# Four graph-attention layers in float32: the tokens of most steps transposed by VectorE in 32x32 blocks after a move across partitions by DMA

## The chip, the core and the metric

The kernel runs on one core of one Trainium2 chip. Five engines work from their own queues, in order: TensorE (PE in the profile; its weight loads are PEld), VectorE (DVE), ScalarE (ACT), GpSimd (POOL) and SyncE (SP), which here only issues DMAs. The metric is the device time of one execution in microseconds; lower is better.

## The reference

There are 8192 tokens of 512 features: 128 graphs of 64 nodes, each graph with its own 64x64 adjacency. Four layers follow each other, each of this form:

```python
h = jnp.maximum(_layernorm(x, axis=-1), 0.0)
x = x + gnn_layer(h, adj, ...)
```

Layers 0 and 2 are attention with 4 heads of 64 (`q = h @ Wq`, `k = h @ Wk`, `v = h @ Wv`, a masked softmax over the 64 nodes of a graph, `out @ Wo + bo`). Layer 1 first normalizes `h` once more with `gamma` and `beta`, and has 8 heads of 64. Layer 3 maps `h` by `map_w`, takes queries and keys from the result, masks the softmax by the cosine similarity of the mapped tokens, and applies it to tokens mapped by another matrix. All of it is float32.

## The kernel before

Work goes in steps of 512 tokens (TB = 4 blocks of 128), 16 steps to a layer, 64 in all; a step is named (l, s). The matrix products want the tokens with features on partitions and tokens along the free axis. A step passes through these stages:

- `loads` (L470): two DMAs of 256 tokens each bring x from DRAM into a tile xin [128 tokens, 2 blocks, 512]; xin has four such tiles (L248). A load of layer l waits for the store of layer l-1 at the same step. SP issues it at L484.
- `layernorms` (L494), one stream for each half: statistics on VectorE (L443, L445), a power on GpSimd (L450), the normalization with ReLU on ScalarE (L459), in place. Layer 1 does this twice.
- `transposes` (L525): TensorE turns 128x128 pieces into PSUM (tile ptr, L539; L516 in layer 1), four pieces to a bank, and ScalarE copies the bank into hT [128 features, 4 chunks, 512 tokens] (L544; in layer 1 L521, which also applies gamma and beta). The xin tile is free when its last transpose is done. There are two hT tiles. Then `has_h` (L557) takes one of the three tiles t [128, 4, 2, 256] for sums of quarters of hT, which GpSimd makes (`sums_of_b`, L356, instruction L366).
- `projections` (L701): each product of a step with a weight matrix is a `winograd` (L633): seven products of quarters in place of eight, on PE at L585, into the PSUM tiles mA, mB, mC. ScalarE evicts (L602, L606, L622), VectorE adds (L615, L626). hT and t are free when all projections that use them are done.
- `scores`, `softmax`, `transposed` (L890 to L953): PE at L902, then VectorE, ScalarE and GpSimd; the probabilities are turned by ScalarE copies of 32-row pieces (L946) and one VectorE transpose in 32x32 blocks (L951).
- `attention` (L1047): PE at L1069, an eviction into a tile of the bank m (L1078), quarter sums by VectorE in another tile of t (L363, called oT_T in the code), and the output product, whose parts are added to the residual. That is read again from DRAM into xres (L992), gets the bias on GpSimd (L996) and the product by L1012 with L1017 or by L615, and is stored at L1037.
- Layer 3 has its own end: `norms` (L828) sends the squared lengths through DRAM and back by small DMAs (L853, L860, L867, L877), and `last` (L1195) multiplies at L1214, adds at L1121 and stores at L1126; its residuals come in at L1107.

All stages are Python generators. A list scheduler (class `Order`, L93) runs them while the program is built: each `yield` names an engine, a duration and a latency, for instance `pe(0.115)` for a transpose or `("sp", 0.6, 3.9)` for a load. It always takes the operation that can start first, and at equal times the stream with the lower priority number (stores 0, attention and residuals 2, transposes 3, loads and layernorms 4, projections 5); it lets urgent streams pass on ACT and DVE. Events hold a stream until something is done, `Ring` hands out tiles in turn, `Bank` gives any free tile to the first who asks. The order of instructions on each engine is fixed by this plan; on the chip an instruction waits for its inputs, and everything behind it on its engine waits too.

The lines that the change touches are mainly these:

```python
pt, pe_ = yield from r_tr.new("ptr")
for c in range(NC):
    yield pe(0.115)
    nc.tensor.transpose(pt[:, c, :], x[:, t, c * P:(c + 1) * P], ident)
```

Of the kernel before, what the change touches and what calls it, by code (L numbers as in the profile page):

```python
# [14 lines left out]
P = 128  # L15
D = 512
N = 64
TB = 4
# [210 lines left out]
def gnn_stack(ctx: ExitStack, tc: tile.TileContext, a: dict, out: bass.AP):  # L229
# [15 lines left out]
    soft = ctx.enter_context(tc.tile_pool(name="soft", bufs=3))  # L245
    dram = ctx.enter_context(tc.tile_pool(name="dram", bufs=1, space=bass.MemoryType.DRAM))
    r_w = ring("w", 4, [P, 7, 2, H])
    r_xin = ring("xin", 4, [P, 2, D])  # L248
    r_xres = ring("xres", 2, [P, 2, D])
    r_u = bank("u", 4, [P, D])  # L250
    r_h = ring("h", 2, [P, NC, TB * P])
# [213 lines left out]

        return lambda j, k: v[:, 2 * j:2 * j + 2, k * H:(k + 1) * H]

    loaded, l_ready = {}, {}

    def loads(steps):  # L470
        for l, s in steps:
            if l > 0:
                yield x_done[l - 1, s]
            for half in range(2):
                v, e = yield from r_xin.new()
                loaded[l, s, half] = v, e

                if (l, s) == (0, 1):
                    if half == 0:
                        yield begun_w  # L480
                    yield ("actq", 0.5, 0.0)
                else:
                    yield load(3.9)
                (nc.scalar if (l, s) == (0, 1) else nc.sync).dma_start(  # L484
                    v, x_of(l, s)[half * H:(half + 1) * H, :].rearrange("(t p) d -> p t d", p=P))
                if (l, s) == (0, 1):
                    if half == 1:
                        loads_begun.set()
                    yield ("actq", 0.0, 8.0)
                l_ready[l, s, half].set()  # L490
# [3 lines left out]
    def layernorms(steps, half):  # L494

        for l, s in steps:
            yield l_ready[l, s, half]
            x, xe = loaded.pop((l, s, half))
            rs = yield from scales(x)
            yield from normalize(x, rs, AF.Relu)  # L500
            if l == 1:
                rs = yield from scales(x)
                yield from normalize(x, rs, AF.Identity)
            normed[l, s, half] = x, xe
            n_ready[l, s, half].set()

    def scaled_chunks(s, h):

        for half in range(2):
            yield n_ready[1, s, half]  # L510
        x = [normed.pop((1, s, half)) for half in range(2)]
        for c in range(NC):
            pt, pe_ = yield from r_tr.new("ptr")
            for b in range(TB):
                yield pe(0.115)
                nc.tensor.transpose(pt[:, b, :], x[b // 2][0][:, b % 2, c * P:(c + 1) * P], ident)  # L516
            if c == NC - 1:
                for _, xe in x:
                    xe.set()
            yield act(0.6)  # L520
            nc.scalar.activation(h[:, c, :], pt.rearrange("p b k -> p (b k)"), AF.Identity,  # L521
                                 bias=beta[:, c:c + 1], scale=gamma[:, c:c + 1])
            pe_.set()

    def transposes(steps):  # L525

        for l, s in steps:
            h, h_done[l, s] = yield from r_h.new("hT")
            hT[l, s] = h
            if l == 1:  # L530
                yield from scaled_chunks(s, h)
            for half in range(2 if l != 1 else 0):
                yield n_ready[l, s, half]
                x, xe = normed.pop((l, s, half))
                for t in range(2):
                    pt, pe_ = yield from r_tr.new("ptr")
                    for c in range(NC):
                        yield pe(0.115)
                        nc.tensor.transpose(pt[:, c, :], x[:, t, c * P:(c + 1) * P], ident)  # L539
                    if t == 1:  # L540
                        xe.set()
                    yield act(0.6)
                    b = 2 * half + t
                    nc.scalar.copy(h[:, :, b * P:(b + 1) * P], pt)  # L544
                    pe_.set()
                if (l, s, half) == (0, 0, 0):
                    yield from has_h(l, s, h)
            if (l, s) == (3, 1):
                yield o_taken
            if (l, s) != (0, 0):  # L550
                yield from has_h(l, s, h)
            yield from sums_of_b(quarters(h), hB[l, s][1], (l, s) == (0, 0))
            hB[l, s][2].set()
            if (l, s) == (0, 0):
                first_t.set()
# [688 lines left out]

    steps = [(l, s) for l in range(4) for s in range(NG)]
    for k in steps:
        for e in (p_ready, s_ready, p_used, h_ready, x_done):
            e[k] = od.event()
        for half in range(2):
            l_ready[(*k, half)], n_ready[(*k, half)] = od.event(), od.event()  # L1250
    with tc.manual_schedule():
        od.spawn(weights(), 4)
        od.spawn(loads(steps), 4)
        for half in range(2):
            od.spawn(layernorms(steps, half), 4)
        od.spawn(transposes(steps), 3)
        od.spawn(projections([k for k in steps if k[0] < 3]), 5)
        od.spawn(fronts(steps), 1)
        od.spawn(turns(steps), 1)
        od.spawn(attentions(steps), 2)  # L1260
        od.run()
# [45 lines left out]
```

## Time and profile before

| | |
|---|---|
| median of 3 runs | 2819.91 us (2817.82 to 2821.3) |
| profiled execution | 2823.6 us, span 2821.8 us |
| PE busy | 2766.3 us (98%), 27176 matmuls |
| DVE busy | 1822.2 us (65%) |
| ACT busy | 1679.4 us (60%) |
| POOL busy | 1539.3 us (55%) |
| DMA | 238.56 MB in 160433 packets, 85 GB/s on average |
| transposes of tokens on PE | L539 x768, L516 x256 |
| granted TensorE clock | 0.995 of full speed |

Busy time is the time in which an engine has an instruction under way; matmuls are pipelined, so a busy PE is not a PE at its peak. The span is that of the profiled execution, from its first instruction to its last. DMA packets are single contiguous pieces; a share of 1 in a window would be all 16 DMA engines busy throughout it. Layer 0 lies at about 0 to 466 us of the span, layer 1 from there to 1400, layer 2 to 1850 and layer 3 to the end; neighbouring layers overlap a little.

### The profile page before, as it was taken

What the parts mean: (1) busy time and instruction counts of PE and PEld (TensorE: products, weight loads), DVE (VectorE), ACT (ScalarE), POOL (GpSimd) and SP (SyncE); (2) the same over time, 40 slices, a digit from 0 to 9 for tenths busy, and PEclk for the clock granted to TensorE, in tenths of its full rate; (3) what the DMA queues carried; (4) which work ended last, traced back from release to release, by engine and by line L of the source; (5) the groups of instructions that cost most, each with busy time, mean ns of one, the idle gap of its engine ahead of it and who ended that gap; (6) DMA issues with size and microseconds to landing.
All of it is one profiled execution on the core that took longest, in us unless ns stands there. A gap on an engine that the chain in (4) does not pass through costs nothing.

```text
span 2821.8 us, 64271 instructions
## 1 busy us (share of the span) xinstructions
PE 2766.3 (98%) x27176; PEld 2398.8 (85%) x27176; DVE 1822.2 (65%) x2724; ACT 1679.4 (60%) x2841; POOL 1539.3 (55%) x1158
## 2 busy tenths in 40 slices
PE   8999999999999999999999999999999999999997
PEld 7888888888888888888889888888888888888876
DVE  6776676776665666655756667646666666665557
ACT  5666666667555755755656657655555555555444
POOL 5676667553444443335565576686545545455443
PEclk9999999999999999999999999999999999999998
DMA  4243233220211111212242233333222322222221
GB/s 156 92 136 100 98 114 129 80 91 29 80 46 69 54 61 47 76 61 77 79 136 99 99 122 107 107 121 85 70 63 82 88 77 62 63 78 75 65 63 46
DMA packets 160433, 238.56 MB, mean 85 GB/s; under 512 B 23953, under 2 KB 69009, under 8 KB 160145
## 3 DMA queue, kind: packets, MB, share of 16 engines
q1 hardware_dynamic: 145632, 219.98, 24.5%
q10 hardware_dynamic: 14512, 14.47, 1.6%
q8 instruction: 214, 3.51, 0.5%
q14 instruction: 75, 0.61, 0.1%
HBM read 166.77 MB, written 67.63 MB: 83 GB/s over the span
## 4 chain that ended last, share of the span: by engine, by line
PE 90%; DVE 4%; POOL 3%; ACT 1%; issue 1%; DMA 1%; POOLq 0%; ACTq 0%; SPq 0%; DVEq 0%
PE mA L585 44%; PE mC L585 22%; PE mB L585 11%; PE sc L902 5%; PE ptr L539 3%; PE po L1069 2%; PE po L1214 1%; PE ptr L516 1%; ACT F L946 1%; POOL t L366 1%; POOL xres L996 1%; PE mmn L844 1%; DVE t L363 1%; POOL E L937 1%; POOL xres L1017 1%
## 5 line engine op out<-in xcount | busy, mean ns | idle before, releaser
L946 ACT COPY F<-E 32x512 f32<-32x512 f32 x768 | 472.5, 615 | 53.7 <-POOL E L937 43.0
L1017 POOL TENSOR_TENSOR xres<-xres,u 128x512 f32<-128x512 f32 x192 | 249.3, 1305 | 207.1 <-ACT u L1012 162.5
L996 POOL TENSOR_TENSOR xres<-xres,u 128x512 f32<-128x512 f32 x192 | 257.0, 1360 | 88.3 <-DMA xres<-x 41.1
L459 ACT ACTIVATE xin<-xin,rs 128x512 f32<-128x512 f32 x320 | 248.6, 811 | 16.7 <-DVE rs L452 15.0
L366 POOL TENSOR_TENSOR t<-hT 128x512 f32<-128x512 f32 x126 | 170.6, 1354 | 144.0 <-ACT hT L544 82.8
L937 POOL TENSOR_TENSOR E<-E,sm 128x1024 f32<-128x1024 f32 x64 | 128.4, 2006 | 201.3 <-DVE sm L935 156.2
L443 DVE BATCH_NORM_STATS2 st<-xin 128x6 f32<-128x512 f32 x320 | 215.2, 672 | 30.1 <-DMA xin<-x 14.3
L602 ACT COPY v<-mA 128x256 f32<-128x256 f32 (+1 forms) x192 | 92.1, 480 | 215.6 <-PE mA L585 201.5
L450 POOL TENSOR_TENSOR rs<-rs,mhalf 128x2 f32<-128x2 f32 x160 | 122.9, 770 | 170.4 <-DVE rs L448 128.8
L585 PE MATMUL mA<-w_vo,t 128*128 128x128 f32 (+1 forms) x1152 | 204.6, 311 | 0.8 <-ACT v L602 0.6
L366 POOL TENSOR_TENSOR t<-hT,t 128x512 f32<-128x512 f32 x126 | 169.7, 1347 | 35.4 <-ACT hT L521 32.2
L585 PE MATMUL mA<-t,w_qk 128*128 128x256 f32 x768 | 185.2, 380 | 2.4 <-DVE t L363 1.4
L931 DVE TENSOR_REDUCE sm<-E 128x16 f32<-128x1024 f32 x128 | 155.2, 1212 | 42.3 <-ACT E L924 41.7
L585 PE MATMUL mA<-t,w_q 128*128 128x256 f32 x744 | 181.2, 380 | 0.9 <-ACT qT L602 0.9
L585 PEld LDWEIGHTS mA<-w_vo,t 128*128 128x128 f32 x1152 | 166.5, 191 | 13.0 <-ACT u L1012 1.8
L585 PE MATMUL mA<-t,w_k 128*128 128x256 f32 x744 | 177.4, 381 | 0.0
L585 PEld LDWEIGHTS mA<-t,w_qk 128*128 128x128 f32 x768 | 142.9, 190 | 21.2 <-issue 1.7
L585 PEld LDWEIGHTS mA<-t,w_k 128*128 128x128 f32 x744 | 140.3, 190 | 19.3
L585 PEld LDWEIGHTS mA<-t,w_q 128*128 128x128 f32 x744 | 137.7, 190 | 20.2 <-issue 2.5
L951 DVE STREAM_TRANSPOSE pt<-F 128x1024 f32<-128x1024 f32 x96 | 118.6, 1235 | 50.5 <-ACT F L946 50.4
L1012 ACT COPY u<-mA 128x512 f32<-128x512 f32 x144 | 84.4, 586 | 107.9 <-PE mA L585 102.2
L937 POOL TENSOR_TENSOR E<-E,f 128x1024 f32<-128x1024 f32 x32 | 63.8, 1994 | 129.9 <-DVE nz L965 65.0
(216 smaller groups left out, 6863.7 us busy)
## 6 DMA issues: line engine op xcount, KB each, us to landing
x<-xres SPq DMA_DIRECT2D x96, 512.0 KB
xin<-x SPq DMA_DIRECT2D x96, 512.0 KB
xres<-x SPq DMA_DIRECT2D x64, 512.0 KB
xres<-in_x SPq DMA_DIRECT2D x32, 512.0 KB
u<-rs SPq DMA_DIRECT2D x128, 128.0 KB
xres<-x SPq DMA_DIRECT2D x64, 256.0 KB
out<-xres SPq DMA_DIRECT2D x64, 256.0 KB
xin<-in_x SPq DMA_DIRECT2D x30, 512.0 KB
```

Source lines behind the costliest of these rows:

```text
L366: nc.gpsimd.tensor_tensor(o, i0, i1, ALU.subtract)
L443: nc.vector.bn_stats(st, v[:, t, :])
L450: nc.gpsimd.tensor_tensor(rs[:, 0, :], rs[:, 1, :], mhalf[:, :2], ALU.pow)
L459: nc.scalar.activation(v[:, t, :], v[:, t, :], func, bias=rs[:, 2, t:t + 1], scale=rs[:, 0, t:t + 1])
L585: nc.tensor.matmul(o, l, r, start=(first and m == 0 and k == 0), stop=(k == KC - 1), skip_group_check=True)
L902: nc.tensor.matmul(S[g * N:(g + 1) * N, par, col], lT[r, c, k], rT[r, c, k], start=True, stop=True)
L931: nc.vector.tensor_reduce(o, E, AX.X, ALU.add)
L937: nc.gpsimd.tensor_mul(E, E, sm[:, :, None].to_broadcast([P, 16, N]))
L946: nc.scalar.copy(F[g * N + 32 * k:g * N + 32 * (k + 1), :, 32 * i:32 * (i + 1)], E[g * N + 32 * i:g * N + 32 * (i + 1), :, 32 * k:32 * (k ...
L951: nc.vector.transpose(o, F)
L996: nc.gpsimd.tensor_add(xr[:, t, :], xr[:, t, :], bo[l])
L1017: nc.gpsimd.tensor_add(v, v, both(u))
```

## The change

In steps 2 to 15 of layers 1, 2 and 3 (42 of the 64 steps) the tokens are no longer transposed by TensorE. Instead:

- A new stream `moves` (priority 3) waits until both halves of a step are normalized, takes a tile t, and issues 16 DMAs on SP from xin into that tile (called F in this role). Each takes 32 partitions and, of each of the 16 pairs of token block and feature chunk, 32 contiguous floats, 128 bytes; it changes the place of a 32x32 block among partitions and columns. The plan counts 0.45 us of SP for each, and 8 us from the issue of the last until it has landed. xin is free after them. In layer 3 an hT tile is taken ahead of the moves; in layers 1 and 2 only when the step is turned.
- `turned_tokens`, called from the stream `transposes`, waits for the moves and turns F into hT with two VectorE transposes in 32x32 blocks, of two token blocks (1024 columns) each.
- In layer 1 ScalarE then applies gamma and beta in place in hT (`scaled`), four instructions of 512 columns.
- The quarter sums of hT are then written into the same tile t over F, by GpSimd as before.
- xin becomes two tiles of four blocks instead of four of two, the same memory; both halves of a step share one.

Steps 0 and 1 of each layer, and all of layer 0, keep the transposes on TensorE.

```diff
-    r_xin = ring("xin", 4, [P, 2, D])
+    r_xin = ring("xin", 2, [P, TB, D])
...
+    by_blocks = [(1, 2), (1, 3), ... (3, 14), (3, 15)]
...
-                v, e = yield from r_xin.new()
-                loaded[l, s, half] = v, e
+                if half == 0:
+                    x, e = yield from r_xin.new()
+                v = x[:, 2 * half:2 * half + 2, :]
+                loaded[l, s, half] = x, e
...
-    def scaled_chunks(s, h):
...
+    def scaled(h):
         for c in range(NC):
-            pt, pe_ = yield from r_tr.new("ptr")
-            for b in range(TB):
-                yield pe(0.115)
-                nc.tensor.transpose(pt[:, b, :], x[b // 2][0][:, b % 2, c * P:(c + 1) * P], ident)
...
-            yield act(0.6)
-            nc.scalar.activation(h[:, c, :], pt.rearrange("p b k -> p (b k)"), AF.Identity,
+            yield act(0.787)
+            nc.scalar.activation(h[:, c, :], h[:, c, :], AF.Identity,
                                  bias=beta[:, c:c + 1], scale=gamma[:, c:c + 1])
-            pe_.set()
+
+    def moves(steps):
+        for l, s in steps:
+            for half in range(2):
+                yield n_ready[l, s, half]
+            if (l, s) == (3, 1):
+                yield o_taken
+            if l not in (0, 1, 2):
+                h, h_done[l, s] = yield from r_h.new("hT")
+                hT[l, s] = h
+            x, xe = normed.pop((l, s))
+            T, t_done[l, s] = yield from r_t.new("T")
+            F = T.rearrange("p c a n -> p (c a n)").rearrange("p (b c i f) -> p b c i f", b=TB, c=NC, i=4)
+            xv = x.rearrange("p b (c k f) -> p (b c) k f", c=NC, k=4)
+            Fv = F.rearrange("p b c i f -> p (b c) i f")
+            for k in range(4):
+                for i in range(4):
+                    yield ("sp", 0.45, 8.0)
+                    nc.sync.dma_start(Fv[32 * k:32 * (k + 1), :, i], xv[32 * i:32 * (i + 1), :, k])
+            xe.set()
+            hB[l, s] = (None, T, od.event())
+            moved[l, s] = F
+            f_ready[l, s].set()
+
+    def turned_tokens(l, s):
+        yield f_ready[l, s]
+        F = moved.pop((l, s))
+        if l in (0, 1, 2):
+            hT[l, s], h_done[l, s] = yield from r_h.new("hT")
+        h = hT[l, s]
+        for b in range(0, TB, 2):
+            yield dve(1.25)
+            nc.vector.transpose(
+                h.rearrange("p c (b n) -> p b c n", b=TB)[:, b:b + 2],
+                F[:, b:b + 2].rearrange("p b c i f -> p b c (i f)"))
+        if l == 1:
+            yield from scaled(h)
+        hB[l, s] = (quarters(h), *hB[l, s][1:])
+        h_ready[l, s].set()
+        return h
...
     def transposes(steps):
         for l, s in steps:
-            h, h_done[l, s] = yield from r_h.new("hT")
-            hT[l, s] = h
-            if l == 1:
-                yield from scaled_chunks(s, h)
-            for half in range(2 if l != 1 else 0):
+            if (l, s) in by_blocks:
+                h = yield from turned_tokens(l, s)
+            else:
+                h, h_done[l, s] = yield from r_h.new("hT")
+                hT[l, s] = h
+            for half in range(0 if (l, s) in by_blocks else 2):
...
+        od.spawn(moves(by_blocks), 3)
```

## The prediction

> **What bounds the kernel now.** I read the page's busy times first, then the chain of work that ended last, then TensorE's waits, then each layer's windows, and then timelines of single steps.
>
> ```profile
> PE 2766.3 (98%) x27176; PEld 2398.8 (85%) x27176; DVE 1822.2 (65%) x2724; ACT 1679.4 (60%) x2841; POOL 1539.3 (55%) x1158
> ```
>
> ```profile
> PE 90%; DVE 4%; POOL 3%; ACT 1%; issue 1%; DMA 1%; POOLq 0%; ACTq 0%; SPq 0%; DVEq 0%
> PE mA L585 44%; PE mC L585 22%; PE mB L585 11%; PE sc L902 5%; PE ptr L539 3%; PE po L1069 2%; PE po L1214 1%; PE ptr L516 1%; ACT F L946 1%; POOL t L366 1%; POOL xres L996 1%; PE mmn L844 1%; DVE t L363 1%; POOL E L937 1%; POOL xres L1017 1%
> ```
>
> TensorE (PE) is 90% of the chain, and its transposes (ptr, L539 and L516) are 3% + 1% of it. PE hardly waits; its longest waits:
>
> ```profile
> PE ptr L539 <- ACT xin L459: 11.5, 1, 11.5
> PE po L1214 <- DVE pt L951: 10.7, 2, 5.7
> PE po L1069 <- DVE E L921: 3.9, 6, 1.1
> PE mB L585 <- DVE xres L615: 3.8, 3, 1.3
> ```
>
> The first is the kernel's start, the second lies in layer 3. All its waits sum to 47 us. So a PE instruction removed is time removed, unless PE then waits for something new. What one transpose is worth is seen in a timeline of PE in layer 1:
>
> ```profile
> 1038.66 0.60 PE L516 MATMUL ptr<-ident,xin 128*128 128x128 f32 x4
> 1039.10 1.46 PE L585 MATMUL mC<-t,w_q 128*128 128x256 f32 x6
> 1040.40 0.60 PE L516 MATMUL ptr<-ident,xin 128*128 128x128 f32 x4
> 1040.83 0.60 PE L585 MATMUL mC<-t,w_q 128*128 128x256 f32 x2
> ```
>
> The start after four transposes comes 0.44 and 0.43 us later (the 0.60 us overlaps the next group). So four cost 0.435 us and one 0.109 us; the busy 119.1 + 40.0 us of all 1024 would overstate it.
>
> The layers differ. Windows for layers 1, 2 and 3 (length, then busy PE, PEld, DVE, ACT, POOL; at the end clock, DMA share, GB/s):
>
> ```profile
> 466.00:1400.00 934.00, 932.94 (x8413) 810.13 (x8411) 588.85 (x909) 570.02 (x877) 429.90 (x338) 1.00 0.20 69
> 1400.00:1850.00 450.00, 441.28 (x4316) 393.98 (x4316) 310.88 (x476) 286.00 (x490) 297.01 (x231) 1.00 0.33 111
> 1850.00:2822.00 972.00, 948.28 (x10157) 800.66 (x10155) 589.72 (x802) 528.13 (x977) 510.38 (x343) 0.99 0.26 73
> ```
>
> With 16 steps to a layer, a step takes 58.4 us in layer 1, 28.1 in layer 2, 60.8 in layer 3. Layer 2 has the least time to hide anything: DVE is at 69%, the DMA engines at 33%, that is 9.3 us of DMA in each 28.1 us step.
>
> **What the Trainium skill says.** "TensorE: Matmul & The Clock Gate", Part 4: PE-mode transpose, gives about 275 ns for a transpose inside one kernel; here the median duration is 273 ns, but the cost in the stream is the 109 ns above. "VectorE: DVE Perf Modes", The three transpose paths: VectorE transposes only 32x32 blocks, each on its own, so blocks must still cross partitions; L951 below agrees in price. "DMA: Bandwidth & Descriptors", Why small descriptors are slow (HBM only): copies from SBUF to SBUF don't suffer the small-packet penalty; no run here shows such a copy. "SBUF — State Buffer", Door 1: 32 neighbouring partitions reach half of the 16 ports; not seen here either, and it would leave about 0.3 us for 64 KB (estimate, half of that page's 436 GB/s), less than what I use below.
>
> **The change, part by part.** It covers 42 steps: steps 2 to 15 of layers 1, 2, 3.
>
> Removed from PE: 42 x 16 = 672 transposes, 168 groups x 0.435 us = **73.1 us**, a third in each layer. All on the path.
>
> ACT: in layers 2 and 3, 28 x 4 PSUM copies (L544, 587 ns) go, 66 us. In layer 1 L521 (780 ns) becomes a scaling in SBUF, for which L459's 811 ns is the nearest: +1.7 us. ACT isn't the bound: I count nothing.
>
> DVE: two transposes of 128x1024 a step. The same operation stands in the page:
>
> ```profile
> L951 DVE STREAM_TRANSPOSE pt<-F 128x1024 f32<-128x1024 f32 x96 | 118.6, 1235 | 50.5 <-ACT F L946 50.4
> ```
>
> 84 x 1.235 = 104 us, 2.5 us a step. In layer 2 DVE goes to (19.4 + 2.5) / 26.4 = 83% of the shorter step (28.1 - 1.74). I count nothing for its busy time, since it lies beside PE; if DVE had no gaps, layer 2 would pay at most 14 x 2.5 = 35 us. The danger is its order: a DVE transpose waits for all 16 moves, and behind it stand the L615 additions that free PE's PSUM banks (0.69 us each).
>
> SP and DMA: 16 moves a step, each 32 partitions x 16 runs of 128 bytes, 512 packets, 64 KB. Issue: plain 256-packet loads take 0.36 us of SP (L992), those of three-part patterns 0.62 (L1107); so 16 x 0.36 to 0.62 = 5.8 to 9.9 us a step. Transfer: nothing moves such packets in bulk, but rn<-ss (L860) is one DMA of 128 packets of 128 bytes. Its landing in windows of 0.05 us:
>
> ```profile
> 2346.25:2346.30 0.05, 0.05 (x2) 0.04 (x1) 0.05 (x1) 0.00 (x0) 0.05 (x1) 1.00 0.55 85
> 2346.30:2346.35 0.05, 0.05 (x2) 0.05 (x1) 0.03 (x1) 0.00 (x0) 0.05 (x1) 1.00 0.46 69
> 2346.35:2346.40 0.05, 0.05 (x2) 0.05 (x1) 0.00 (x0) 0.00 (x0) 0.05 (x1) 1.00 0.61 92
> ```
>
> Over its whole landing (0.30 us at a share of 0.36) it keeps an engine busy 0.108 us for 8 packets: 13.5 ns each. Low end: 512 packets for each engine a step x 13.5 ns = 6.9 us. At the burst's 85 GB/s, 1.05 MB take **12.3 us**, which I take, as the engines weren't full in it. High end: a 128-byte packet as dear as one of 2 KB, 89 ns (2048 bytes at 369 GB/s over 16 engines, in a full stretch at 1061 us): 45 us. With about 1.2 us from issue (2345.26) to the last byte, a step's moves last 13.5 us. The planner writes 16 x 0.45 + 8 = 15.2 us, so its order fits.
>
> The waits on SP: moves wait for ACT's normalization and for a free t buffer, that is for PE's projections of an earlier step. Queued behind them are stores, xres loads, masks, and layer 3's norm transfers; for them wait POOL (L996, L885), then DVE and PE. In layer 1 and 3 each has tens of us: an xres load issued at 1022 us serves an output unit whose first eviction (L1012) is at 1048. In layer 2 xres loads issued at 1678.8 and 1680.6 are first added to at 1684.1 (L996), and POOL meets L1017 at 1691.2: some 7 us of slack against a backlog of 12.3 - 7.2 = 5 us.
>
> Buffers: t (three tiles) is now taken before the moves. In layer 2 a tile was held about 48 us (1645 to 1693); by need it is now 13.5 moves + 2.5 DVE + 5.3 POOL + 27.6 projections = 49 us, plus oT_T's 21 us (1682 to 1704). 70 us on three tiles allow a step of 23.3 us; PE wants 26.4. A tile freed when a projection ends (1693) gives sums at about 1714, while PE comes for them at about 1720: 5 to 6 us spare. In layers 1 and 3 a step of 57 to 59 us leaves 20 us and more. xin: a slot is held for load and normalization, 24 us (L484 at 1678, last L459 at 1702), and for the moves, 13.5 us, together 37.5 against 2 x 26.4.
>
> So layers 1 and 3 keep 48.7 us. In layer 2 a thin margin (5 us) shared by DMAs that vary by several us will sometimes break; I take 1 us a step, 14 us, from 0 (always hidden) to 4 us a step, 56. Sum: -73 + 15 (one for the tail) = -58. Against the profiled execution's 2823.6 us (2821.8 of span and 1.8 around it) that is 2765.6; it lay 3.7 us above the median of the runs, so I predict **2762 us**.
>
> **Rivals.**
> 1. *Slower: the DMA queue becomes layer 2's bound.* Its 26.4 us step leaves 26.4 - 9.3 = 17.1 us for moves; each us more costs 14 us in all, so 73 us are eaten at 17.1 + 5.2 = 22.3 us a step, 44 ns a packet. At 26 us the loss is 14 x 8.9 = 125 us: 2820 - 73 + 125 = 2872. For: the bulk rate is unknown and the high end is 45 us. Against: 13.5 ns in the burst.
> 2. *The gain of layer 2 is lost to a new wait.* If moves interleave with the 9.3 us of other traffic, or hold the third t tile when oT_T wants it, DVE or POOL stands 4 us a step: 56 us, so 2820 - 73 + 56 = 2803. For: the thin margin, and DVE's 83%. Against: 7 us of slack in xres.
> 3. *Nothing changes*, because PE's place was not on the path. Against: 47 us of waits in 2821.8; it would give 2820. Hardly possible.
>
> **How the numbers follow.** Forecast 0.60 (its own range 2742 to 2788), rival 2 with 0.18 (to 2815), rival 3 with 0.02, rival 1 with 0.20 (from 2826, mostly 2835 to 2930). The range from 2740 (all 73 us and a little of waits) to 2836 leaves out most of rival 1 and little else. About 0.2% (5.6 us) is what a measurement can tell. Faster 0.77, same 0.03, slower 0.20.
>
> **What would show it.** Right: PE with 26504 matmuls, L951's kind of operation at 84 more of about 1.24 us, layer 1 near 910 us, layer 3 near 948, layer 2 at 426 to 440, PE's waits under 70 us. Moves: 0.4 to 0.8 us of SP each, DMA share 0.37 to 0.45. Wrong: SP held 1.5 us or more by each move, a DMA share above 0.9 in layer 2, DVE's new transposes idle before a DMA for more than 100 us in sum, or PE waiting on L615 and t for over 70 us.

## The result and the profile after

The changed kernel takes 2835.29 us (median of 5 runs, 2830.69 to 2841.34) against 2819.91 us: a ratio of 1.0055, 95% interval 1.0043 to 1.0067. It is slower by some 15 us, where 58 us less were forecast. The 672 transposes did leave TensorE (PE). What they were worth, and 15 us more, came back as waiting and as a lower clock. (In the tables below one execution of run 11, at 2988.4 us in a slower state, is left out; with it the median of run 11 is 2785.5 us, the figure that a later expectation uses.)

The change moves the line numbers: L585 becomes L619, L615 becomes L649, L539 becomes L576, L921 becomes L955, L996 becomes L1030, L1012 becomes L1046 and L1214 becomes L1248; the moves are issued at L536 and turned at L551. In the runs with four wide moves most are one higher.

The page's busy times and its chain of work that ended last, changed kernel:

```profile
PE 2722.7 (96%) x26504; PEld 2352.6 (83%) x26504; DVE 1894.1 (67%) x2808; ACT 1618.1 (57%) x2729; POOL 1543.6 (54%) x1158
...
PE 79%; DVE 6%; SPq 4%; DMA 4%; POOL 3%; issue 2%; ACT 2%; POOLq 0%; ACTq 0%; DVEq 0%
```

PE has its 26504 matmuls, but its part of the chain fell from 90% to 79%, and SP's queue and DMA, which had 1% together, now have 8%. PE's longest waits (engine, tile, line, what it waited for; us in total, times, longest):

```profile
PE sc L936 <- DVE E L955: 15.8, 10, 2.5
PE ptr L576 <- ACT xin L459: 13.3, 2, 11.4
PE mA L619 <- ACT u L1046: 13.0, 4, 4.0
PE po L1248 <- DVE pt L985: 10.7, 2, 5.7
PE mA L619 <- POOL t L366: 10.3, 2, 8.0
```

The second and fourth were there before. The first lies in layer 3, the third and fifth in layer 2; these three waits are for VectorE, ScalarE and GpSimd in turn.

For the layers I cut the span at the first and last start of layer 1's products of hT with w_q and at layer 2's last product of w_vo with hT. Layers 1, 2 and 3 so cut, before and then after (window and length, then busy PE, PEld, DVE, ACT, POOL; at the end PE's granted clock, DMA share, GB/s):

```profile
479.20:1309.30 830.10, 829.04 (x7444) 718.23 (x7443) 521.93 (x816) 512.17 (x782) 372.06 (x291) 1.00 0.18 62
1309.30:1826.80 517.50, 510.76 (x4965) 455.69 (x4965) 350.89 (x531) 319.11 (x544) 327.14 (x257) 1.00 0.32 108
1826.80:2821.80 995.00, 969.50 (x10323) 818.40 (x10321) 606.41 (x828) 544.88 (x1006) 530.69 (x360) 0.99 0.26 74
```

```profile
479.00:1279.80 800.80, 797.01 (x7118) 688.52 (x7118) 542.96 (x838) 505.44 (x772) 359.00 (x286) 1.00 0.32 82
1279.80:1854.90 575.10, 530.50 (x4959) 465.21 (x4958) 383.08 (x566) 300.68 (x505) 339.20 (x267) 0.95 0.48 129
1854.90:2832.90 978.00, 938.98 (x10001) 792.59 (x9999) 633.56 (x856) 511.25 (x945) 535.76 (x356) 0.98 0.38 88
```

Layer 1 gained 29 us and layer 3 gained 17, but layer 2 is 58 us longer. Layer 2's row gives two reasons: PE is idle for 44.6 us of it (6.7 before), and its clock is 0.95. The layers overlap at the cuts, so a row tells where to look, and only whole spans are compared exactly: in run 2 below, where layer 2 is not changed, its row is 543.8 us long, so up to 26 of the 58 us are layer 1's work that now falls behind the cut.

The span is PE's busy time plus its idle time, and this closes the account. Before: 2766.3 + 55.5 us. After: 2722.7 + 110.2. Without 73.1 us of transposes, busy time should be 2693.2; it is 29.5 us more, at a clock of 0.983 in place of 0.995. So -73.1 + 29.5 + 54.7 = +11.1 us, which is the difference of the spans, 2832.9 - 2821.8. The clock is about enough to explain the 29.5 us: 2693.2 x (0.995 / 0.983 - 1) = 33 us (an estimate from these figures).

The lower clock goes with the idle time. The Trainium skill, "TensorE: Matmul & The Clock Gate", Why this matters for your kernels, warns that a gap of more than about 3 us between bursts of matmuls drops TensorE to half its clock. The timeline of a stall in layer 2 of the changed kernel agrees (start, us, what; in brackets the idle time and what ended it):

```profile
1580.16 1.89 PE L619 MATMUL mB<-hT,w_qk 128*128 128x256 f32 x8
1590.01 3.78 PE L619 MATMUL mA<-t,w_qk 128*128 128x256 f32 x8 [7.96 <-POOL t L366]
1593.76 1.79 PE L1103 MATMUL po<-pt,v 64*64 64x64 f32 x64
1595.48 1.99 PE L619 MATMUL mC<-t,w_qk 128*128 128x256 f32 x8
```

Eight matmuls take 1.89 us before the gap of 7.96 us and 3.78 us after it; the granted clock from 1590.0 to 1593.8 us was 0.50. What PE waits for there is in POOL's and SP's timelines:

```profile
1559.97 6.25 SPq L536 DMA_DIRECT2D t<-xin  x8
1566.27 0.62 SPq L1026 DMA_DIRECT2D xres<-x  x1
1566.93 4.47 SPq L536 DMA_DIRECT2D t<-xin  x5
...
1571.22 2.49 POOL L1030 TENSOR_TENSOR xres<-xres,u 128x512 f32<-128x512 f32 x2 [8.27 <-DMA xres<-x]
```

The residual load (L1026) is issued behind eight moves, POOL stands 8.27 us for it at L1030, and the sums L366 that PE wants come after that in POOL's order, at 1587.34. This reading suggested that the moves' hold on SP in layer 2 was the whole cause. It was not.

### The profile page after: what moved, and what is told of

Its sections match the earlier page's. It is cut to its first block, busy times and chain, and to the rows that moved or that the text cites. A ratio compares the mean times of both kernels' runs of the same rounds, so it can differ in the third digit from the quotient of the medians.

```text
span 2832.9 us, 63998 instructions
## 1 busy us (share of the span) xinstructions
PE 2722.7 (96%) x26504; PEld 2352.6 (83%) x26504; DVE 1894.1 (67%) x2808; ACT 1618.1 (57%) x2729; POOL 1543.6 (54%) x1158
## 3 DMA queue, kind: packets, MB, share of 16 engines
q1 hardware_dynamic: 500448, 264.07, 35.6%
## 4 chain that ended last, share of the span: by engine, by line
PE 79%; DVE 6%; SPq 4%; DMA 4%; POOL 3%; issue 2%; ACT 2%; POOLq 0%; ACTq 0%; DVEq 0%
PE mA L619 40%; PE mC L619 20%; PE mB L619 10%; PE sc L936 4%; PE po L1103 2%; DMA xin<-x 2%; SPq L536 2%; SPq L911 1%; PE ptr L576 1%; ACT F L980 1%; PE po L1248 1%; DVE E L955 1%; DVE st L443 1%; POOL E L971 1%; DVE sc L947 1%
## 5 line engine op out<-in xcount | busy, mean ns | idle before, releaser
L1030 POOL TENSOR_TENSOR xres<-xres,u 128x512 f32<-128x512 f32 x192 | 254.0, 1343 | 195.2 <-DMA xres<-x 182.1
L459 ACT ACTIVATE xin<-xin,rs 128x512 f32<-128x512 f32 x320 | 248.3, 809 | 27.9 <-DVE rs L452 26.7
L366 POOL TENSOR_TENSOR t<-hT 128x512 f32<-128x512 f32 x126 | 176.9, 1404 | 155.0 <-DMA u<-rs 92.1
L443 DVE BATCH_NORM_STATS2 st<-xin 128x6 f32<-128x512 f32 x320 | 215.1, 673 | 53.3 <-DMA xin<-x 45.3
L619 PE MATMUL mA<-w_vo,t 128*128 128x128 f32 (+1 forms) x1152 | 206.0, 314 | 13.0 <-ACT u L1046 13.0
L636 ACT COPY v<-mA 128x256 f32<-128x256 f32 (+1 forms) x192 | 91.8, 478 | 213.6 <-PE mA L619 198.3
L619 PE MATMUL mA<-t,w_qk 128*128 128x256 f32 x768 | 194.9, 395 | 13.1 <-POOL t L366 10.3
L619 PEld LDWEIGHTS mA<-w_vo,t 128*128 128x128 f32 x1152 | 168.6, 193 | 27.5 <-ACT u L1046 16.4
L619 PEld LDWEIGHTS mA<-t,w_qk 128*128 128x128 f32 x768 | 150.1, 199 | 36.1 <-POOL t L366 11.1
L619 PE MATMUL mA<-t,w_q 128*128 128x256 f32 x744 | 179.2, 383 | 0.6 <-ACT qT L636 0.6
L619 PE MATMUL mA<-t,w_k 128*128 128x256 f32 x744 | 179.1, 381 | 0.0
L366 POOL TENSOR_TENSOR t<-hT,t 128x512 f32<-128x512 f32 x126 | 171.5, 1361 | 6.2 <-ACT hT L514 2.7
L619 PEld LDWEIGHTS mA<-t,w_q 128*128 128x128 f32 x744 | 140.2, 191 | 22.2 <-issue 2.7
L1046 ACT COPY u<-mA 128x512 f32<-128x512 f32 x144 | 84.2, 585 | 128.9 <-PE mA L619 118.1
L619 PEld LDWEIGHTS mA<-t,w_k 128*128 128x128 f32 x744 | 140.3, 190 | 19.4
```

Of the source, the lines that this page charges most:

```text
L366: nc.gpsimd.tensor_tensor(o, i0, i1, ALU.subtract)
L443: nc.vector.bn_stats(st, v[:, t, :])
L459: nc.scalar.activation(v[:, t, :], v[:, t, :], func, bias=rs[:, 2, t:t + 1], scale=rs[:, 0, t:t + 1])
L619: nc.tensor.matmul(o, l, r, start=(first and m == 0 and k == 0), stop=(k == KC - 1), skip_group_check=True)
L1030: nc.gpsimd.tensor_add(xr[:, t, :], xr[:, t, :], bo[l])
```

## The experiments

Times are medians; each ratio is to executions of the kernel before on the same chip and at the same time (their medians lay between 2820.7 and 2823.1 us). The columns from the span on are of the profiled execution. Runs 4, 7 and 14 to 17 are given in the text only.

| run | us | ratio (95%) | span | PE busy | PE idle | idle in layers 1 / 2 / 3 |
|---|---|---|---|---|---|---|
| before | 2819.91 | | 2821.8 | 2766.3 | 55.5 | 1.1 / 6.7 / 25.5 |
| changed | 2835.29 | 1.0055 (1.0043-1.0067) | 2832.9 | 2722.7 | 110.2 | 3.8 / 44.6 / 39.0 |
| 1: layers 1, 3 | 2820.69 | 1.0000 (0.9989-1.0011) | 2817.9 | 2730.2 | 87.8 | 4.4 / 10.4 / 51.0 |
| 2: layer 1 | 2809.36 | 0.9953 (0.9937-0.9970) | 2808.0 | 2744.4 | 63.6 | 3.6 / 11.2 / 26.7 |
| 3: 1 KB pieces | 2815.10 | 0.9980 (0.9972-0.9988) | 2817.7 | 2713.7 | 104.0 | 3.4 / 43.3 / 35.2 |
| 6: 0.67 us in plan | 2834.26 | 1.0054 (1.0034-1.0074) | 2829.1 | 2717.3 | 111.8 | 9.0 / 36.4 / 44.1 |
| 5: four wide moves | 2813.71 | 0.9976 (0.9963-0.9989) | 2812.0 | 2716.3 | 95.7 | 3.9 / 34.3 / 35.3 |
| 10: turn on ACT | 2830.35 | 1.0038 (1.0025-1.0050) | 2826.4 | 2718.3 | 108.0 | 11.2 / 39.8 / 34.8 |
| 8: whole slots only | 2836.29 | 1.0048 (1.0033-1.0063) | 2832.7 | 2768.1 | 64.6 | 0.2 / 14.5 / 26.8 |
| 9: layer 1, half slots | 2820.21 | 0.9996 (0.9988-1.0005) | 2817.0 | 2745.6 | 71.4 | 14.4 / 8.1 / 27.6 |
| 11: layers 1, 3, late stats | 2782.96 | 0.9869 (0.9852-0.9885) | 2786.3 | 2723.8 | 62.5 | 3.6 / 9.6 / 26.8 |
| 12: all, late stats | 2810.09 | 0.9959 (0.9944-0.9974) | 2806.5 | 2710.4 | 96.1 | 4.0 / 48.0 / 22.0 |
| 13: before, late stats | 2819.93 | 0.9994 (0.9986-1.0003) | 2818.8 | 2765.3 | 53.5 | 1.2 / 6.8 / 22.8 |
| 18: short path | 2782.09 | 0.9856 (0.9839-0.9872) | 2781.6 | 2706.3 | 75.3 | 3.7 / 19.8 / 29.2 |

In every kernel that is built from the changed one, steps 0 and 1 of layer 1 go through PE without the scaling by gamma and beta, as in the change itself; these are 1 and 0 in the inputs. Runs 3, 5, 10 and 18 leave out the transposition of the moved tokens in part or whole and serve as experiments only.

**Where it is lost.** The first theory (A) was that layer 2 loses it all.

```
-    by_blocks = [(1, 2), (1, 3), ... (3, 15)]
+    by_blocks = [(l, s) for l in (1, 3) for s in range(2, 16)]    # run 1
+    by_blocks = [(1, s) for s in range(2, 16)]                    # run 2
```

> Moves only in layers 1 and 3; layer 2 keeps its transposes on TensorE. Theory A (the whole loss arises in layer 2, whose 26 us step is too short for the moves on SP; layers 1 and 3 keep their gains, which the two traces put at 30 and 17 us): 2770 to 2785 us. Theory B (the moves cost something in every layer, through the longer DMA queue): above 2800 us.

> Only layer 1 by blocks (14 steps, 224 transposes less), the moves on SP; layers 2 and 3 go through TensorE as in the kernel before, but with the two whole input slots. Worth 24.4 us if nothing new is waited for: 2797 us, TensorE idle for 55 to 60 us. Theory Q (SP held by moves, harmless where a step lasts 57 us and nothing on SP is urgent): 2795 to 2803 us. Theory E (coarser input slots cost time in layer 3, moves or not): 2810 to 2830 us, with VectorE's statistics waiting for xin in layer 3 as in the run with layers 1 and 3.

Theory A fell: layers 1 and 3 alone gain nothing. Layer 1 alone gains 13 us of its 24.4, between what theories Q and E said. Adding layer 3 then costs 11 us, though it takes 24.4 us from PE; adding layer 2 costs 15 more. So, taken in this order, layer 1 loses some 11 us, layer 3 some 36 and layer 2 some 39. Together that is 86 us against 73, which is the result.

**SP and the transfers.** Three runs change what the moves cost SP and the DMA engines.

```
# run 3: the same 16 moves, with pieces of 1 KB in place of 128 bytes
-    nc.sync.dma_start(Fv[32*k:32*(k+1), :, i], xv[32*i:32*(i+1), :, k])
+    nc.sync.dma_start(Fw[32*k:32*(k+1), :, i], xw[32*i:32*(i+1), :, k])
# run 4: each move cut in two
+    for j in range(2):
+        r = slice(8*j, 8*j+8)
+        yield ("sp", 0.225, 8.0)
+        nc.sync.dma_start(Fv[32*k:32*(k+1), r, i], xv[32*i:32*(i+1), r, k])
# run 5: four moves over 128 partitions, none across partitions
+    for i in range(4):
+        yield ("sp", 1.8, 8.0)
+        nc.sync.dma_start(Fw[:, :, i], xw[:, :, i])
```

> The same plan, the same 16 DMAs a step with the same 64 KB and the same waits, but each partition's 2 KB go as two pieces of 1 KB in place of sixteen of 128 bytes, so the tokens arrive in the wrong places and the output is not the reference's. Theory A (the 128-byte packets make each move hold SP 0.63 us and more, and so delay the xres loads queued behind): SP held about 0.4 us a move, layer 2 regained, 2750 to 2775 us. Theory C (layer 2 lacks a third free tile of t, or the plan's order itself is bad): 2815 us or more, as the packets do not matter then.

> Each move cut in two: 32 DMAs a step of 256 packets of 128 bytes, the plan counts 0.225 us each, so 7.2 us a step as before. If the packets set the pace (512 packets in 0.63 us): SP is held about 0.33 us a move, 10 to 11 us a step, and the time stays at 2825 to 2850 us. If each DMA costs SP 0.6 us whatever its size: 19 us a step, layer 2 is far longer, above 2950 us.

> All 42 steps as in the changed kernel, with the same bytes, buffers, waits, VectorE transposes and planned SP time (4 x 1.8 us and 8 us of transfer), but a step's data go in 4 DMAs over all 128 partitions in place of 16 DMAs over 32. They don't cross partitions, so the tokens of these steps are not transposed and the output is not the reference's; everything else is computed as before. The plain loads over 128 partitions held SP 0.36 us each, so SP should be held about 1.5 us a step in place of 9.4. Theory Q (what delays the rest is the time that SP is held): TensorE's idle time falls from 110 us to 70 us or less and the time to 2750 to 2775 us. Theory B (the buffers t and xin, VectorE's order or the plan): idle time stays over 95 us and the time at 2810 us or more. If SP is held 0.6 us for each of the four and the time is between, the transfer itself counts.

The line of the moves in the changed kernel, then in the run with four wide ones (count, duration ns min/median/max, first and last start):

```profile
L536 SPq DMA_DIRECT2D t<-xin x672: 585/632/2223, 556.0 to 2671.7; - x168
```

```profile
L537 SPq DMA_DIRECT2D t<-xin x168: 593/632/1530, 553.3 to 2638.9; - x168
```

A move holds SP about 0.63 us whether it covers 32 partitions and 512 packets or 128 partitions and 256. Cut in two, each half still held it 0.61 us, and that kernel took 3197 us in its one execution: here the price went by the number of DMAs. Yet 4 x 0.63 us a step in place of 16 x 0.63 brought no more than wide pieces alone did: 2813.7 against 2815.1 us. The two have in common a shorter transfer, worth some 20 us. Theory Q, that SP's hold delays the rest, fell as the main cause; most of the loss was left in both.

Two other edits on SP's side brought nothing. One told the plan 0.67 us for a move in place of 0.45; the other took run 1, with layers 1 and 3 by blocks, and issued its moves from ScalarE.

```
-    yield ("sp", 0.45, 8.0)
+    yield ("sp", 0.67, 8.0)                                  # run 6
+    yield ("act", 0.6, 8.0); nc.scalar.dma_start(...)        # run 7
```

> The plan counts 0.67 us of SP for each move, as measured, in place of 0.45; the work is the same, only the order on the engines is planned anew. Theory A: the plan now puts xres loads and what hangs on them where they can be served, about half of layer 2's 80 us comes back, 2785 to 2810 us. Theory D (the DMA engines or buffers are simply full in layer 2, whatever the order): above 2825 us.

> Only layers 1 and 3 by blocks, as in the earlier run of that form, which took 2820.7 us with TensorE idle for 88 us; the 16 moves of a step are issued from ScalarE's queue in place of SP's, at a planned 0.6 us each. SP is then as free as in the kernel before, while ScalarE stands some 0.6 us for each of its 448 moves (about 270 us beside 1647 us of work in 2818 us). Theory Q (SP held by the moves delays loads and residual loads): TensorE's idle time falls to 60 us or less, and the time to 2770 to 2790 us. Theory E (input slots or order, not SP): idle time stays near 85 us or more and the time at 2815 us or more. A third outcome would show ScalarE as the new wait: TensorE waiting for ACT xin, u or F by over 40 us, time above 2825 us.

Run 6 gave 2834.3 us, the changed kernel's time, as theory D said. Run 7 gave 2881.8 us (ratio 1.0206, 1.0190 to 1.0221) against run 1's 2820.7: TensorE's idle time rose to 126 us, with 38.0 us of L1248 waiting for VectorE's L955. It is slower than either theory said, and not by the waits that the third outcome named, so it doesn't tell the theories apart.

**The input slots.** The change also turned four half slots of xin into two whole ones. One run does only that to the kernel before, another undoes it with layer 1 by blocks.

```
-    r_xin = ring("xin", 4, [P, 2, D])
+    r_xin = ring("xin", 2, [P, TB, D])         # run 8, in the kernel before
-                    if t == 1:
+                    if t == 1 and half == 1:
                         xe.set()
# run 9: two tiles, whose halves have events of their own again
+    x = xins[k // 2 % 2]; v = x[:, 2*half:2*half+2, :]
```

> The kernel before with one part of the change alone: the input buffer has two whole tiles in place of four half tiles, so that a slot comes free only after the last transpose of a step, and a load must wait for that. TensorE still transposes everything, and nothing is moved between partitions. Theory E (the coarser input slots make the loads late, and with them the norms, in layer 3 above all): TensorE's idle time rises from 55 us by 15 us or more, and the time is 2835 to 2860 us. Theory Q (the moves on SP's queue delay what is queued behind them; the slots are innocent): within 4 us of the kernel before, 2817 to 2825 us, and idle time of TensorE 50 to 60 us.

> Layer 1 alone by blocks (2809.4 us with whole input slots), with the four half slots of the kernel before restored: two adjacent tiles whose halves are freed one by one where TensorE transposes, and together where a step is moved. Theory E (the whole slots cost 14 us, in layers 2 and 3, whatever else is done): 2793 to 2798 us. If the cost of the slots and that of the moves don't add: 2805 to 2812 us.

Alone, the whole slots cost 14 us, as theory E said, though PE's idle time rose by 9 us and not by 15; I took this for a fixed price. With half slots layer 1 by blocks got slower by 11 us, not faster by 14: idle time rose by 10.8 us in layer 1, nearly all of it at its start, and fell by 3.1 us in layer 2. So the slots have no fixed price that could be added or taken off. Each edit makes the planner write another order, and that alone can move the time by several us (by 8 in run 15 below, where one figure of the plan is all that differs). The 11 us of layer 1 in run 2 are hardly larger, and no run explains them.

**VectorE's load.** In the run with four wide moves, the two turns of a step become plain copies on ScalarE.

```
-    nc.vector.transpose(h.rearrange(...), ...)
+    nc.scalar.copy(h.rearrange(...), ...)       # run 10
```

> The run with four wide moves (2813.7 us; TensorE idle 95.7 us, 34 of them in layer 2), and the two instructions of a step that turned blocks on VectorE are plain copies on ScalarE, at the same places of the order that the plan wrote. They turn nothing, so that the tokens of the 42 steps are not transposed within a block either and the output is not the reference's. VectorE is relieved of 84 x 1.24 = 104 us, ScalarE gets some 90 us. Theory D (VectorE's load and order is what delays layer 2): TensorE's idle time falls by 20 us or more, to below 76 us, the time to 2790 us or less. Theory C (the path from load to sums is too long in its buffers and its order, whichever engine turns): idle time stays within 10 us of 95.7 us and the time at 2805 to 2825 us, since ScalarE, too, takes its work in order.

It took 2830.4 us, 17 more than with VectorE, and PE's idle time rose by 12 us. So theory D's gain did not come. ScalarE got 78 us of work in exchange, so the run doesn't show what VectorE's turns would be worth if no engine had to do them.

**Layer 3.** The loss is easiest to see in the run with layers 1 and 3. First a step of the kernel before (SP's input load and u loads, VectorE's statistics L443 and masks L921), then a step of that run:

```profile
2119.81 4.22 SPq L484 DMA_DIRECT2D xin<-x  x2
2129.48 5.74 SPq L877 DMA_DIRECT2D u<-rs  x8
...
2124.32 0.68 DVE L443 BATCH_NORM_STATS2 st<-xin 128x6 f32<-128x512 f32 x1
2148.51 1.22 DVE L921 TENSOR_TENSOR E<-sc,mx 128x1024 f32<-128x1024 f32 x1
```

```profile
2101.61 11.46 SPq L536 DMA_DIRECT2D t<-xin  x16
2117.54 5.63 SPq L911 DMA_DIRECT2D u<-rs  x8
2124.65 1.91 SPq L487 DMA_DIRECT2D xin<-x  x2
...
2130.47 0.69 DVE L443 BATCH_NORM_STATS2 st<-xin 128x6 f32<-128x512 f32 x1 [3.17 <-DMA xin<-x]
2137.19 1.21 DVE L955 TENSOR_TENSOR E<-sc,mx 128x1024 f32<-128x1024 f32 x1
...
2138.55 1.98 PE L936 MATMUL sc<-kT,qT 64*64 64x64 f32 x64 [2.49 <-DVE E L955]
```

Before, the input load went out ahead of the u loads, and the statistics ran some 20 us before the masks. Now the slot comes free only when the moves are done, in the plan 8 us after the last is issued, and the load goes out after the u loads; the statistics stand 3.17 us for it with the masks behind them, and PE waits 2.49 us for the masks, after which its 64 matmuls take 1.98 us in place of 1.16 (granted clock from 2138.5 to 2140.6 us: 0.50). From one input load to the next a step lasts 61.8 us (2124.65 to 2186.43); before it was 59.0. The whole slots alone don't do this: in run 8 VectorE stood only 1.3 us in all before such loads in layer 3. The tokens of that load aren't moved until two steps on: nothing but the written order makes it urgent. The plan reckons 3.9 us for the load to land. The next runs say 12 us, in layer 3 only, and change nothing else.

```
-                    yield load(3.9)
+                    yield load(12.0 if l == 3 else 3.9)
# run 11: with layers 1 and 3; run 12: all 42 steps; run 13: the kernel before
```

> The run with layers 1 and 3 by blocks (2820.7 us; TensorE idle 88 us, of which L936 behind L955 22 us; VectorE's L443 behind the input load 34 us in layer 3), and in layer 3 alone the plan is told that an input load lands after 12 us in place of 3.9. No instruction is added or removed; VectorE's order then has the masks (L955) ahead of the statistics of the next tokens (L443). Theory S (in layer 3 the loss comes from VectorE standing in its order before a load that the moves have made late): the wait of L936 for L955 falls below 6 us, TensorE's idle time by 12 us or more, the time to 2795 to 2808 us. If the cause in layer 3 is the wait for t or the DMAs themselves: unchanged within 5 us, 2816 to 2826 us.

> The changed kernel, all 42 steps by blocks (2835.3 us), with one figure of the plan altered: in layer 3 an input load is told to land after 12 us in place of 3.9. No instruction is added or removed. The same figure took the form with layers 1 and 3 from 2820.7 to 2785.5 us. Theory S (layer 3's loss is VectorE standing in its order before a late load, independent of layer 2): some 25 to 40 us less than the changed kernel, 2795 to 2812 us, with layer 2 as slow as before (idle 44 us). If layer 3 was late because layer 2 hands it on late: 2825 to 2840 us.

> Control: the kernel before, with the same figure of the plan (an input load of layer 3 lands after 12 us in place of 3.9), nothing else. There, VectorE stood 14 us in all before these loads and TensorE 3 us behind L921. Theory S (the figure mends what the moves did): within 6 us of the kernel before, 2814 to 2826 us. If the plan's figure is wrong for any form of this kernel, and so has nothing to do with the moves: 2785 to 2805 us.

With it, VectorE has the masks ahead of the statistics. VectorE's wait for the load in layer 3 of run 1, the first line below, is gone in run 11. PE's waits for the masks follow, in run 1 (whole span) and in run 11 (layer 3's window):

```profile
DVE st L443 <- DMA xin<-x: 35.4, 17, 4.0
```

```profile
PE sc L936 <- DVE E L955: 22.2, 10, 2.8
```

```profile
PE sc L936 <- DVE E L955: 2.1, 2, 1.6
```

Layers 1 and 3 by blocks go from 2820.7 to 2783.0 us, more than expected, and all 42 steps from 2835.3 to 2810.1. The kernel before doesn't change (ratio 0.9994), so it is the change that made the figure wrong. Against layer 1 alone, layer 3 now gains 26 us, where its transposes were priced at 24.4. Of the 24 us by which PE's idle time in layer 3 fell, 20 are its wait for the masks. So theory S is shown as the cause in layer 3; that the time fell 12 us below its range is not explained. Run 11 is also the fastest version that computes the reference: 1.3% under the kernel before.

**Layer 2.** With that mended, layer 2 by blocks costs 27 us (2783.0 to 2810.1) where 24.4 us of transposes should be gained: some 51 us are lost in 14 steps. Four runs alter the plan or the buffers of the run with all 42 steps.

```
+    yield load(12.0 if l == 2 else 4.6)          # run 14: residual loads, layer 2
+    yield load(12.0 if l in (2, 3) else 3.9)     # run 15: input loads, layer 2 too
-    r_t = bank("t", 3, ...)    +    r_t = bank("t", 4, ...)      # run 16
-    r_qk = ring("qk", 3, ...)  +    r_qk = ring("qk", 2, ...)    # runs 16 and 17
```

> As the changed kernel with the altered figure for layer 3's input loads, and in layer 2 the plan is told that a residual load lands after 12 us in place of 4.6, so that GpSimd's order need not have the additions to it (L1030) ahead of the sums (L366) that TensorE waits for. Theory P (in layer 2 the loss comes from GpSimd standing in its order before residual loads that the moves have made late): GpSimd's wait of L1030 for xres falls from 195 us by half, TensorE's idle time in layer 2 from 44 us by 15 us or more, the time 15 to 30 us under the run without it. If the length of the path itself bounds layer 2: within 6 us of the run without it.

> As the changed kernel with the altered figure for input loads, in layers 2 and 3 both. In layer 2 of the changed kernel VectorE's L443 waited 16 us for input loads, three times, once 10.5 us. If that is what delays layer 2: TensorE's idle time there falls from 44 us by 10 us or more, and the time is 10 to 20 us under the run with layer 3's figure alone. If GpSimd's order (theory P) or the length of the path is the cause: within 6 us of that run, or slower.

> The changed kernel with layer 3's altered load figure (2810.1 us; layer 2 lasts 575 us there, TensorE idle 48 us in it), with four t tiles in place of three; the 8 KB for it are taken from the qk buffer, which has two tiles in place of three. To be read against the run with two qk tiles and three t tiles. Theory T (in layer 2 the moves wait for a free t tile, and so the sums come late): 15 us or more under that run. Otherwise within 6 us of it, or slower.

> The control for the run with four t tiles: two qk tiles in place of three, three t tiles, all else as there. What a missing qk tile costs shows against 2810.1 us; I expect 0 to 40 us, since qk tiles are held from the projection to the scores.

Run 14 took 2942.1 us (ratio 1.0419, 1.0401 to 1.0436): the remedy made a worse order, with PE waiting 141 us for ScalarE's L636, and in layer 2 GpSimd's L1030 waited not less but more for residual loads, 151 us in place of 86.5 in run 12. That alone doesn't refute theory P, but the run with four wide moves speaks against it: there POOL's L1031 (L1030 in the changed kernel) waited only 22 us for residual loads in layer 2, and PE still stood 34 us. In run 15 VectorE's waits for input loads in layer 2 are gone, PE is idle 50.0 us there (48.0 without), and the time, 2818.1 us, is 8 us longer, so late input loads are not layer 2's cause. Run 16 took 2830.4 us (ratio 1.0033, 1.0021 to 1.0044), its control 2819.8 (0.9992, 0.9983 to 1.0001). With four t tiles PE's idle time in layer 2 fell from 51.4 to 45.8 us and rose elsewhere, so a lack of t tiles is at most a small part, and theory T fell as the main cause.

What was left to try is the length of the path. The moves put some 13 us of issue and transfer on the chip, and 15.2 us in the plan, between the norm and the sums. In the run with four wide moves the transfer was short, but the plan still reckoned 15.2 us. A step of it:

```profile
1585.51 3.52 SPq L537 DMA_DIRECT2D t<-xin  x4
...
1603.19 1.24 DVE L552 STREAM_TRANSPOSE hT<-t 128x1024 f32<-128x1024 f32 x1
```

The last of the four was issued by 1589.0; VectorE turned at 1603.2, without a wait before it. The last run tells the plan what these moves take.

```
-                yield ("sp", 1.8, 8.0)
+                yield ("sp", 0.65, 2.0)          # run 18
```

> The run with four wide moves (2813.7 us; TensorE idle 96 us, 34 of them in layer 2; output not the reference's, since the tokens of the 42 steps aren't moved across partitions), and the plan is told what these four moves take, 4 x 0.65 us and 2 us to land, in place of 4 x 1.8 and 8 us. There, the moves of layer 2 had landed about 10 us before VectorE came to turn them at its place in the order. Theory L (what layer 2 loses beyond the packets is the 15 us that moves add, in the plan as on the chip, to the path from the norm to the sums): VectorE turns 8 to 12 us earlier, TensorE's idle time in layer 2 falls from 34 to 20 us or less, and the time to 2775 to 2800 us. If the buffers (t, hT) set layer 2's pace whatever the path: within 6 us of 2813.7 us.

The time is 2782.1 us, and PE is idle for 19.8 us in layer 2 in place of 34.3, both as theory L expected. PE's longest waits in run 5 and in run 18 (those for L366, L986 and L637 lie in layer 2):

```profile
PE mA L620 <- ACT u L1047: 14.9, 6, 4.0
...
PE mA L620 <- POOL t L366: 10.2, 3, 5.4
PE sc L937 <- DVE E L956: 8.5, 10, 2.5
PE po L1104 <- DVE pt L986: 5.8, 2, 4.0
PE mC L620 <- ACT qk L637: 4.3, 3, 2.9
```

```profile
PE mA L620 <- ACT u L1047: 15.9, 4, 4.3
...
PE sc L937 <- DVE E L956: 1.6, 1, 1.6
```

In run 18 the waits for the sums (L366), of the attention product (L1104) for the turned probabilities (L986) and for L637 are gone. But the other half of the expectation did not come: over the 14 steps of layer 2 the time from the first move to the turn is 18.3 us by median in run 5 and 20.8 us in run 18. In some steps the turn came nearer (moves from 1494.2, turn at 1499.9), in others not (1566.9 and 1587.2), since the moves themselves go out earlier. So the run shows that planning these moves as longer than they are costs some 30 us. It doesn't show that the length of the path on the chip is the cause in layer 2. Part of the gain isn't layer 2's either: in layer 3 PE's wait for the masks (L956) fell from 8.5 to 1.6 us. In layer 2 GpSimd's wait for residual loads rose to 57 us while PE waited less, which speaks against theory P once more. And not all is regained there: 15.9 of the 19.8 us are four waits for ScalarE's L1047, of about 4 us each, which the kernel before doesn't have (its wait for the same copy, L1012, is 0.2 us). This kernel doesn't transpose; the changed kernel's own moves take about what its plan says, and no run gives it another figure for their landing. What turns them into waits in layer 2 stays open.

## Why the prediction was wrong

By its own steps:

- *The transposes, 73.1 us, all on the path.* Right as a price: layer 1 alone lowered PE's busy time by 21.9 us of 24.4, and with the late statistics layer 3 gained 26 where 24.4 were priced. That it would stay gained was the error.
- *ACT and DVE at nothing.* Not contradicted for their busy time: VectorE's 84 turns took 1225 ns each and stood idle 0.9 us in all, and handing them to ScalarE brought nothing. VectorE's order mattered, but by the statistics, not by the turns, where I had looked for the danger.
- *Issue, 0.36 to 0.62 us of SP.* The upper end: 0.63 us, 10 us a step.
- *Transfer, 12.3 us a step.* Good in size: 16 moves were issued in 11.5 us in layer 3, so the issue set the pace. That VectorE's turns hardly waited for the last to land says little, since the plan had put them late. The queue's share of the 16 engines' time rose from 24.5% to 35.6%, that is 1008.5 - 691.3 = 317 us of all 16 engines, or 7.6 us a step in 42 steps, near the low end of 6.9. Rival 1 (the DMA queue becomes the bound) is out: the DMA share in layer 2 is 0.48. But the page of the Trainium skill that frees SBUF-to-SBUF copies of the small-packet penalty ("DMA: Bandwidth & Descriptors", Why small descriptors are slow (HBM only)) doesn't hold here: with 1 KB pieces the same bytes took 904.5 - 691.3 = 213 us, and the kernel 20 us less (904.5 is run 3's share, 32.1% of its span).
- *"The planner writes 16 x 0.45 + 8 = 15.2 us, so its order fits", and "layers 1 and 3 keep 48.7 us".* This is the step that failed for layer 3. I compared the plan's figure for the moves with the moves' own duration. I didn't ask what else the plan places by them: the xin slot now comes free after the moves, so the next input load goes out later, and the statistics and the masks stand behind it on VectorE. I had counted the slot's time (37.5 us against two steps) and found room, and there is room; the order leaves it unused. Layer 3 lost some 36 us by it where I had nothing. Layer 1 lost some 11 us, also put at nothing; no run explains these.
- *Layer 2, 1 us a step.* This is the term that was mis-sized: the loss was 39 us (run 1 to the changed kernel) to 51 us (run 11 to run 12), or 2.8 to 3.7 us a step, within the bound of 4 that I gave. A margin did break, but not shown to be the one I named: the t tiles are at most a small part (runs 16 and 17), and the backlog on SP is not the main cause (run 5), nor is GpSimd's wait for xres (runs 5 and 18). Rival 2 is nearest in size, a new wait of 4 us a step in layer 2; which buffer or engine makes it stays open. Between forecast and result lie 73 us: layer 3's 36, layer 1's 11 and the 25 by which layer 2's 39 exceed my 14.
- *PE's clock* was missing from the sum. Waits in a stream of matmuls are paid more than once: with 54.7 us more of idle time came 29.5 us more of busy time.
- *What would make it wrong.* None of the four signs came: a move held SP 0.63 us, the DMA share stayed under 0.5, the turns didn't wait, and PE's waits for L649 (L615 before) and t are far under 70 us. Of the signs of being right, PE's waits under 70 us failed: it was idle for 110 us. I had named large single waits; the loss came in many waits of a few us each, on several engines.

## What to carry to other kernels

When work is taken from the engine that is the bound and sent a longer way round, list what comes free later because of it (here an input slot) and whose place in which engine's order was written with the old time; the latency on that way can count even where no engine and no queue is full. Here a wait of the bound engine cost more than itself, as its clock fell in the gap. And where a planner writes the order, run the kernel before with the same plan figure as a control, since a new order alone moved the time here by 8 us (run 15) and more.

## What the runs showed of the hardware that I had not expected

A copy from SBUF to SBUF with strided patterns on both sides held SP 0.60 to 0.63 us, whether it covered 32 or 128 partitions and 64 to 512 packets, while plain loads of the kernel before took 0.36 us. (Its loads and stores of three-part patterns, L1107 and L1126, also took 0.62 us, so it need not be a matter of SBUF.) The same bytes in 128-byte packets took the DMA engines half as long again as in 1 KB packets, 317 us against 213. After a gap of 7.96 us eight matmuls ran at half their rate (3.78 us in place of 1.89), and after one of only 2.49 us, shorter than the 3 us above, 64 small ones took 1.98 us in place of 1.16; the granted clock was 0.50 in both.
